# Convolution and attention on one core: bulk transfers on GpSimd's queue, 18 diagonal products in place of 36, norm sums a slot earlier

## The chip, the cores and the metric

The kernel runs on one core of a Trainium2 chip. The metric is the device time in microseconds (us); the time before is the median of three runs. A core has five engines with a queue of instructions each: PE (TensorE, matrix products), DVE (VectorE), ACT (ScalarE), POOL (GpSimd) and SP (SyncE, used here for transfers only). Transfers are issued from the queues of SP, ACT and POOL and are carried out by the core's 16 DMA engines.

## What is computed

The reference takes images x of 4 x 384 x 48 x 48 and does this (shortened):

```python
x_flat = x.reshape(B, C, N).transpose(0, 2, 1)
local = conv7x7_per_channel(x, conv_w) * inv + (bn_beta - bn_mean * inv)
x_norm = layernorm(x_flat)
q, k, v = heads(x_norm @ qkv_w.T + qkv_b)
q = q + heads(layernorm(local_flat))
attn = softmax(q @ k.T * 48 ** -0.5)
out = x_flat + (attn @ v) @ proj_w.T + proj_b
```

There are N = 2304 tokens of C = 384 channels in an image, and 8 heads of 48. So there are a depthwise convolution of 49 taps, two layer norms over channels, three projections, attention of every token with every token of its image, and an output projection with a residual.

## The kernel before

**Tiles.** An image is cut into six groups of 8 rows (384 tokens), so there are 24 tiles t = 6b + g. Heads are taken in four pairs. Channels lie on the partitions in three chunks of 128 (heads 0 to 5 fill 48 of each 64 rows, heads 6 and 7 fill the other 16 in thirds).

**Slots.** The attention of a tile has 12 slots, three for each pair of heads. A slot (`score_batch`, `weigh_batch`, lines 925 to 938) scores six blocks of 128 keys (`score`, line 897: six products of 64 rows each for a block, L902, then an exponential on ACT, L910) and weighs the values with the result (`weigh`, L917). After the last slot, `sums_out` copies the sums to SBUF on ACT (L802, L812) and `sums_add` adds the thirds on DVE (L821).

**Between images** comes a key stage: for each of six groups, `from_x` (line 588) projects values, keys and queries of the next image and the output of the image before (all L529). Keys are split in a high and a low part; `keys_out` (line 556) sends them in pieces, for pair 0 to the SBUF stack `ks` on SP's queue, for the others to `wide` in HBM on POOL's queue. `load_keys` (line 582, L586) brings a pair's keys back in thirds on POOL's queue; there are two `ks` buffers, and a load of the next pair waits until PE has read the last key of the pair before the present one.

**Convolution.** DVE does the taps (`conv_ops`, line 263; L289, the first one L285), one instruction for a tap and chunk. They run one tile ahead of attention. `plan` (line 377) spreads them over the points between other work: each point has an estimate of DVE's room there (`spare`, `spare_at_keys`) and each tile a due point (`due`). For the first two tiles some taps of chunk 0 are done on PE, as products with diagonals (`products`, L304): 10 taps for tile 0, `MORE_TAPS` for tile 1, whose diagonals `make_more` (line 312) writes into buffers that are not yet in use. Products stand ahead of an ACT copy into the accumulator (L1047), and after that come the first tile's `query_end`, `high_queries` and `low_queries`.

**Norms.** Class `Norm` sums over channels. In the first image's tiles the mean comes from PE (`mean_kept`). Elsewhere `sum` adds the chunks on DVE (L422, L423) and `out` (line 473) transposes, reduces, and sends the sums in two hops over HBM on SP's queue (`parts` L482, `four` L483), since the four partial sums lie on different partitions. `few_centre` and `few_variance` take them up on DVE (L492, L500, L506); then come the squares on ACT (L417, run in `weigh_batch` ahead of the weighing) and the same again for the variance. The norm of the local part of the next tile runs in slots `first - 1` to `second + 1` (5 and 8), that of the coming image's x around `X_SLOTS`.

**Queries.** `high_queries` rounds a pair's queries on ACT (L774), `low_queries` takes the difference on DVE (L779) and sends six hops within SBUF on SP's queue (L784, L786), after which the scores of that pair can start. `gather_tails` (line 531, L535) collects the tails of the queries for pair 3 in eight hops.

**Queues.** The order on PE, DVE and ACT is the order of the source. On SP and POOL the scheduler of the framework sets the order of transfers at build time, so it has to be read from the built kernel. On SP's queue there lie, beside the hops, the slabs of the convolution (`load_slab`), the tiles of x (`load_x`), the residuals (`load_residual`), and the outputs held in HBM until the key stage (`hold`, `fetch`). A finished tile is divided by its sums (`divide`, slot 2) and multiplied and held at `OUT_SLOT`.

Of the kernel before, what the change touches and what calls it, by code (L numbers as in the profile page):

```python
# [25 lines left out]
NSLOT = 12  # L26
X_SLOTS = 4, 7
X_LATER = 3
OUT_SLOT = 4
WARM = 14  # L30
PE_TAPS = 10
MORE_TAPS = 36

# [11 lines left out]
def unshifted_pass(  # L47
# [16 lines left out]
    nc = tc.nc  # L64
    B, C, N = x.shape
    W = 48
# [26 lines left out]
    def load_packed(dst, src, queue=nc.sync):  # L93
        for p0, piece in segments(src):
            queue.dma_start(out=dst[p0 : p0 + piece.shape[0]], in_=piece)
# [4 lines left out]
    def place_x(b, g):  # L100
        xn[b, g] = big.tile([P, CC, G], F32, tag=f"xn{g}", name=f"xn{b}_{g}")
        return xn[b, g]

    def load_x(b, g):
        load_packed(place_x(b, g), x[b, :, g * G : (g + 1) * G])

    slabs = {}

    def load_slab(b, g, parts=1):
        first, end = max(0, g * RG - PAD), min(H, (g + 1) * RG + PAD)  # L110
        t = work.tile([P, CC, (RG + 2 * PAD) * W], F32, tag="slab", name=f"slab{b}_{g}")

        edges = (first, (g + 1) * RG, end) if parts == 2 else (first, end)
        for a, e in zip(edges, edges[1:]):
            load_packed(t[:, :, (a - first) * W : (e - first) * W], x[b, :, a * W : e * W])
        slabs[b, g] = (t, first, end)


# [57 lines left out]
                    )  # L176

    load_by_pair(of_ln, ln_pair, (nc.scalar, nc.gpsimd))
    load_slab(0, 0, parts=2)
    place_x(0, 0)  # L180
    nc.gpsimd.tensor_scalar_add(inv, norms[:, 3], BN_EPS)
    nc.gpsimd.tensor_tensor(inv, inv, neg_half, ALU.pow)
# [50 lines left out]
    load_packed(staged[1], qkv_wT[:, C : 2 * C])  # L233
    load_packed(staged[0], qkv_wT[:, 0:C])
    for g in range(1, NG):
        load_x(0, g)
    load_by_pair(qk_vec, qk_b, (nc.gpsimd, nc.gpsimd))
    with nc.allow_non_contiguous_dma(reason="a few vectors, once"):
        load_packed(vbp, v_b.rearrange("o c -> c o"), nc.gpsimd)
# [70 lines left out]
        return more[i // 9][:, i % 9 * P : i % 9 * P + P]  # L310

    def make_more():
        for tag, bufs in (("qs", 5), ("qs", 5), ("ao", 2), ("rb", 1)):
            d = work.tile([P, CC, G], F32, tag=tag, name="more", bufs=bufs)
            more.append(d.rearrange("p c g -> p (c g)"))
            for i in range(9 * len(more) - 9, 9 * len(more)):
                nc.scalar.mul(more_diagonal(i), ident, cw[:, 0, taps[i] : taps[i] + 1])
            yield
# [5 lines left out]
    def norm_slots(t):  # L324
        return (8 - (t > 0), None) if t + 1 < NG else (5, 8)

    def spare(t, s, half):
        b, g = divmod(t, NG)
        first, second = norm_slots(t)
        time = 3.6 - (0.0 if half else 0.6) - (0.6 if half and s % 3 == 1 else 0.0)  # L330
        if b + 1 < B and g >= later(b + 1):
            time -= {(3, 1): 2.3, (4, 1): 2.2, (5, 1): 2.3, (7, 0): 0.4, (8, 0): 2.6}.get(
                (s, half), 0.0
            )
        if g:
            time -= {(2, 0): 0.7, (4, 1): 1.4}.get((s, half), 0.0)
        if t + 1 < NG:
            time -= {(first + 1, 0): 1.4, (first + 2, 0): 4.3, (first + 3, 0): 0.6}.get(
                (s, half), 0.0
            )  # L340
        elif g < NG - 1:
            time -= {(4, 1): 2.3, (5, 1): 2.2, (6, 1): 2.3, (8, 0): 0.4, (9, 0): 4.5}.get(
                (s, half), 0.0
            )
        return max(0.3, time)
# [23 lines left out]
    each = CC * KS * KS  # L369
    due = []  # L370
    for t in range(1, NT):
        last = ("slot", t - 1, norm_slots(t - 1)[0], t < NG) if t % NG else ("kv", t, 4, 0)
        due.append((points.index(last), t * each - MORE_TAPS))
    share = {}

# [279 lines left out]
    def both(making):  # L655
        next(making)
        next(making)

    def lows_out(n):
        for _ in range(n):  # L660
            lows.popleft()()
# [92 lines left out]
    def query_end(t):  # L754

        acc = accs.pop(t)
        q = xn[divmod(t, NG)]
        q3 = work.tile([P, G], F32, tag="qt", name=f"qt{t}", bufs=1)
        queries[t] = q, q3
        for c in range(CC):  # L760
            nc.vector.scalar_tensor_tensor(
                q[:, c, :], acc[:, c, :], gain[:, c : c + 1], q[:, c, :], ALU.mult, ALU.add
            )
# [7 lines left out]
    def high_queries(t, p):  # L771
        qs = work.tile([P, 3, G], HALF, tag="qs", name=f"qs{t}_{p}", bufs=5)
        stacked[t, p] = qs
        nc.scalar.copy(qs[:, 0, :], query_of(t, p))  # L774

    def low_queries(t, p):

        qs = stacked[t, p]
        nc.vector.tensor_sub(qs[:, 1, :], query_of(t, p), qs[:, 0, :])  # L779
        qs = qs.bitcast(F32)  # L780
        for j in range(2):
            r = 64 * j
            if p < CC:
                nc.sync.dma_start(out=qs[r + HD : r + 64, 0:2], in_=qs[r : r + 16, 0:2])  # L784
            for i in range(2):
                nc.sync.dma_start(  # L786
                    out=qs[r + 32 * i : r + 32 * i + 32, 2], in_=qs[r + 16 : r + HD, i]
                )
# [69 lines left out]
    def load_residual(t, tag="qs", bufs=5):  # L858
        b, g = divmod(t, NG)
        xr = work.tile([P, CC, G], F32, tag=tag, name=f"xr{t}", bufs=bufs)  # L860
        nc.sync.dma_start(
            out=xr, in_=x[b, :, g * G : (g + 1) * G].rearrange("(c p) n -> p c n", p=P)
        )
        residuals[t] = xr
# [2 lines left out]

    def hold(t):
        held[t] = dram.tile([P, CC, G], F32, tag=f"held{t % NG}", name=f"held{t}", bufs=1)
        nc.sync.dma_start(out=held[t], in_=outputs[t][0])  # L870

    def fetch(t):
        if t < NT - NG:
            ao = work.tile([P, CC, G], F32, tag="qs", name=f"af{t}", bufs=5)
        else:
            ao = big.tile([P, CC, G], F32, tag=f"xn{t % NG}", name=f"af{t}")
        nc.sync.dma_start(out=ao, in_=held[t])
        return ao

    def finish(t, co, m, queue=nc.sync):  # L880
# [44 lines left out]
    def score_batch(t, s):  # L925
        p, k0 = s // (KB // BATCH), s % (KB // BATCH) * BATCH
        for kb in range(k0, k0 + BATCH):
            score(t, p, kb)
# [17 lines left out]
    def convolve_first(n):  # L946
        nonlocal n_first
        n_first += n
        for _ in range(n):
            next(stream)  # L950
# [62 lines left out]
    for g in range(1, NG):  # L1013

        last = g == NG - 1
        next(making_more, None)
        making = from_x(0, g)
        both(making)
        assert not last or n_first >= each - PE_TAPS
        norm = Norm(accs[0] if last else xn[0, g + 1])  # L1020
        norm.mean_by_chunk(norm.src)
        if last:
            added = output_bias()
        convolve_first(4)
        norm.centre()
        norm.squares()
        both(making)
        if not last:
            convolve_first(4)
            both(making)  # L1030
        norm.mean_by_chunk(norm.buf)
        norm.root()
        lows_out(1)
        if last:
            both(making)
        both(making)
        convolve_first(6 if last else 10)
        if not last:
            lows_out(2)
        if last:  # L1040
            local_end(0, norm.newton())
        else:
            norm.scale(norm.newton())
        both(making)
        if not last:
            convolve_first(7)
    nc.scalar.activation(  # L1047
        accs[1][:, 0, :], products(1, MORE_TAPS, more_diagonal), AF.Identity, bias=shift[:, 0:1]
    )
    query_end(0)  # L1050
    high_queries(0, 0)
    low_queries(0, 0)
    lows_out(2)
    gather_tails(*reversed(queries[0]))
    nc.vector.tensor_add(pb, pb, added)
    plan(n_first - (each - PE_TAPS))

    for t in range(NT):
        b, g = divmod(t, NG)
        if g == 0 and b:  # L1060
# [4 lines left out]
            for gk in range(NG):  # L1065
# [40 lines left out]
                    norm.squares()  # L1106
                if gk == 5:
                    low_queries(t, 0)
                    gather_tails(*reversed(queries[t]))
                both(making)  # L1110
                convolve("kv", t, gk, 3)
                lows_out(2)
# [18 lines left out]
        for s in range(NSLOT):  # L1131
# [3 lines left out]
            if early and s == first + 3:  # L1135
                high_queries(t + 1, 0)
            score_batch(t, s)
            if pair < NP - 1 or g < NG - 1:
                load_keys(b, (pair + 1) % NP, third)
            if s == 1 and g == 0:  # L1140
# [29 lines left out]
                norm.few_variance()  # L1170
            if early and s == first + 3:
                low_queries(t + 1, 0)
                gather_tails(*reversed(queries[t + 1]))
            convolve("slot", t, s, 0)
            sums_add()
            if early and s == first + 1:
# [18 lines left out]
            convolve("slot", t, s, 1)  # L1195
            if following and s == second + 1:
                low_queries(t + 1, 0)
                gather_tails(*reversed(queries[t + 1]))
            if coming and s == X_SLOTS[0]:
                norm_x.few_centre()  # L1200
            if following and s == first:
# [1 line left out]
            if s == OUT_SLOT and g:  # L1203
                ao = outputs[t - 1][0]
                nc.vector.tensor_mul(ao, ao, rb)
                hold(t - 1)
            if coming and s == X_SLOTS[0] - 1:
                norm_x = Norm(xn[b + 1, g - later(b + 1)])
                norm_x.sum()
                norm_x.out()  # L1210
            if coming and s == X_SLOTS[0] + 1:
                norm_x.sum_squares()
                norm_x.out()
            if following and s == first - 1:
                norm = Norm(accs[t + 1])
                norm.sum()
                norm.out()
# [562 lines left out]
```

## Time and profile before

| what | us |
|---|---|
| median of three runs | 2858.78 |
| lowest and highest | 2855.7 and 2859.26 |
| the profiled execution: own time | 2871.85 |
| the profiled execution: span of its instructions | 2870.1 |
| PE busy in the span | 2802.3 |
| DVE busy | 2419.7 |
| ACT busy | 1653.8 |
| POOL busy | 592.4 |

The profile is of one execution, whose own time lies 13.1 us above the median. "PE" is the time in which products run, "PEld" the loading of weights beside it. A row of waits reads: engine, what it was to do and the line, what it waited for, total us, number of times, longest. A row of the timeline reads: start and length in us, engine, line, operation, output and inputs, number of records, and in brackets the idle time ahead of it with what ended it. SPq is the transfer queue of SP. A product of 32-bit floats shows as two records. The three key stages lie near 750, 1464 and 2150 us, the tiles' slots between them.

### The profile page before, as it was taken

What the parts mean: (1) busy time and instruction counts of PE and PEld (TensorE: products, weight loads), DVE (VectorE), ACT (ScalarE), POOL (GpSimd) and SP (SyncE); (2) the same over time, 40 slices, a digit from 0 to 9 for tenths busy, and PEclk for the clock granted to TensorE, in tenths of its full rate; (3) what the DMA queues carried; (4) which work ended last, traced back from release to release, by engine and by line L of the source; (5) the groups of instructions that cost most, each with busy time, mean ns of one, the idle gap of its engine ahead of it and who ended that gap; (6) DMA issues with size and microseconds to landing.
All of it is one profiled execution on the core that took longest, in us unless ns stands there. A gap on an engine that the chain in (4) does not pass through costs nothing.

```text
span 2870.1 us, 53777 instructions
## 1 busy us (share of the span) xinstructions
PE 2802.3 (98%) x19366; PEld 1757.3 (61%) x19366; DVE 2419.7 (84%) x4783; ACT 1653.8 (58%) x2677; POOL 592.4 (21%) x1125
## 2 busy tenths in 40 slices
PE   9999999999999998999999999999999999999999
PEld 6655666666655655655665566666565566666665
DVE  7759899989899887988989999989888999988502
ACT  5436666666424665666642476666662266666662
POOL 5720000000274100000036400001006610110000
PEclk9999999999999999999999999999999999999999
DMA  6434544554455444445545554454455545535541
GB/s 141 108 111 137 146 136 138 152 154 152 112 154 163 144 132 146 138 132 154 153 117 155 168 165 144 144 149 145 135 151 151 136 161 158 147 136 169 165 160 62
DMA packets 195348, 410.33 MB, mean 143 GB/s; under 512 B 67776, under 2 KB 138368, under 8 KB 194560
## 3 DMA queue, kind: packets, MB, share of 16 engines
q0 software_dynamic: 65440, 254.88, 26.4%
q1 hardware_dynamic: 126640, 148.30, 21.5%
q8 instruction: 155, 2.54, 0.4%
q10 hardware_dynamic: 2992, 3.62, 0.4%
q14 instruction: 121, 0.99, 0.1%
HBM read 298.25 MB, written 64.73 MB: 126 GB/s over the span
## 4 chain that ended last, share of the span: by engine, by line
PE 72%; DVE 15%; DMA 8%; ACT 1%; issue 1%; POOL 1%; SPq 1%; ACTq 0%; DVEq 0%
PE o L917 30%; PE r L902 25%; PE r L529 16%; DVE acc L289 9%; DMA four<-parts 2%; DMA qs<-qs 1%; DMA parts<-part 1%; PE r L304 1%; DVE sq L478 1%; DMA wide<-k 0%; DVE sq L423 0%; ACT pt L910 0%; DVE part L479 0%; DVE sq L422 0%; DMA slab<-in_x_dram 0%
## 5 line engine op out<-in xcount | busy, mean ns | idle before, releaser
L289 DVE SCALAR_TENSOR_TENSOR acc<-slab,vec,acc 128x368 f32<-128x368 f32 (+4 forms) x3412 | 1751.6, 585 | 1.6
L910 ACT ACTIVATE pt<-r 128x768 f32<-128x768 f32 x1728 | 1248.8, 829 | 115.8 <-PE r L902 92.0
L917 PE MATMUL o<-pt,v 128*64 128x384 f32 x6912 | 1181.9, 491 | 1.9 <-ACT pt L910 1.8
L902 PE MATMUL r<-qs,ks 64*128 64x384 f32 x10368 | 1010.6, 343 | 56.1 <-ACT ao L812 26.0
L902 PEld LDWEIGHTS r<-qs,ks 64*128 64x128 f32 x10368 | 900.7, 187 | 244.8 <-issue 178.6
L917 PEld LDWEIGHTS o<-pt,v 128*64 128x64 f32 x6912 | 471.5, 137 | 592.7 <-issue 515.2
L586 POOL DMA_DIRECT2D ks<-wide x276 | 199.3, 724 | 1811.6 <-PE r L902 1781.6
L802 ACT COPY o<-o 113x384 f32<-113x384 f32 x192 | 92.0, 479 | 388.5 <-PE o L917 388.5
L529 PE MATMUL r<-xn,w_qk 128*128 128x384 f32 x864 | 283.7, 486 | 0.0
L529 PEld LDWEIGHTS r<-xn,w_qk 128*128 128x128 f32 x864 | 164.2, 190 | 114.5
L529 PE MATMUL r<-w_v,xn 128*128 128x384 f32 x432 | 145.1, 488 | 0.5 <-ACT w_v L715 0.5
L606 ACT COPY v<-r 128x384 f32<-128x384 f32 x72 | 32.1, 480 | 186.2 <-PE r L529 186.2
L821 DVE TENSOR_TENSOR ao<-ao,o 113x384 f32<-113x384 f32 x144 | 79.7, 554 | 50.8 <-ACT o L802 50.5
L529 PE MATMUL r<-af,w_o 128*128 128x384 f32 x360 | 119.1, 487 | 0.0
L529 PEld LDWEIGHTS r<-w_v,xn 128*128 128x128 f32 x432 | 81.5, 190 | 59.1 <-issue 2.4
L492 DVE TENSOR_REDUCE few<-four 128x12 f32<-128x48 f32 x72 | 16.7, 232 | 117.1 <-DMA four<-parts 117.1
L812 ACT COPY ao<-o 113x384 f32<-113x384 f32 x72 | 34.4, 478 | 131.9 <-PE o L917 131.9
L529 PEld LDWEIGHTS r<-af,w_o 128*128 128x128 f32 x360 | 68.2, 190 | 47.8 <-issue 0.6
L554 POOL DMA_DIRECT2D wide<-k x192 | 96.5, 507 | 2.9 <-issue 2.6
L576 POOL DMA_DIRECT2D wide<-k x192 | 92.8, 489 | 11.4 <-DMA wide<-k 9.6
L570 POOL DMA_DIRECT2D wide<-k x144 | 70.8, 495 | 101.9 <-ACT k L614 70.1
L779 DVE TENSOR_TENSOR qs<-xn,qs 128x384 fp32r<-128x384 f32 x72 | 39.9, 554 | 55.9 <-ACT qs L774 55.8
(131 smaller groups left out, 1224.9 us busy)
## 6 DMA issues: line engine op xcount, KB each, us to landing
ks<-wide POOLq DMA_DIRECT2D x276, 768.0 KB, 6.8
qs<-qs SPq DMA_DIRECT2D x528, 48.0 KB
xr<-in_x_dram SPq DMA_DIRECT2D x24, 576.0 KB
slab<-in_x_dram SPq DMA_DIRECT2D x32, 378.0 KB
wide<-k POOLq DMA_DIRECT2D x480, 24.0 KB, 2.0
held<-ao SPq DMA_DIRECT2D x20, 576.0 KB
af<-held SPq DMA_DIRECT2D x20, 576.0 KB
rb<-rden SPq DMA_DIRECT2D x48, 216.0 KB
```

What stands on the lines that cost most here:

```text
L289: nc.vector.scalar_tensor_tensor(dst, src, weight, dst, ALU.mult, ALU.add)
L529: nc.tensor.matmul(dst, lhsT=weights(c), rhs=src(c), start=c == 0, stop=c == CC - 1)
L554: queue.dma_start(out=dst[r + 32 * i : r + 32 * i + 32, 1], in_=k[r + 16 : r + HD, 1])
L570: nc.gpsimd.dma_start(out=last[16 * u : 16 * u + 16, 0], in_=k[r : r + 16, 0])
L576: nc.gpsimd.dma_start(out=last[to : to + 16, 1], in_=k[r : r + 16, 1])
L586: nc.gpsimd.dma_start(out=stacks[b, p].bitcast(F32)[:, :, at], in_=wide[b, p][:, :, at])
L779: nc.vector.tensor_sub(qs[:, 1, :], query_of(t, p), qs[:, 0, :])
L802: nc.scalar.copy(part[0 : 64 + HA], sums[0 : 64 + HA, 0, :G])
L821: nc.vector.tensor_add(dst, dst, part[0 : 64 + HA])
L902: nc.tensor.matmul(r[:, j, :G], lhsT=ks[rows, w, kb * P : (kb + 1) * P], rhs=qs[rows, m, :], start=i == 0, stop=i == 2,)
L910: nc.scalar.activation(pt, r[:, :, :G], AF.Exp, scale=SCALE)
L917: nc.tensor.matmul(sums[halves[j], 0, :G], lhsT=values[t // NG, kb // NB][:, first : first + 64], rhs=pt[:, j, :], start=i == 0, stop=i == ...
```

## The change

Bulk transfers (slabs, x, residuals, held outputs) go from SP's queue to POOL's, except those of the start; the small hops, the denominators' broadcast (`rb`) and the output of finished tiles stay on SP. Tile 1 has 18 taps done as products in place of 36, and the first tile's query work stands ahead of these products. Both norms' first sums are formed one slot earlier, and the room estimates and due points follow. The tails are gathered in slot 0, after its scores, in place of directly after the first query hops. The finished tile is multiplied and held in slot 7 in place of 4. Below, the line with `dma_start` stands for the three of `load_residual`, `hold` and `fetch`; the block with `both(making)` is the end of the start-up; `gather_tails` is no longer called elsewhere.

```diff
-OUT_SLOT = 4
+OUT_SLOT = 7
-MORE_TAPS = 36
+MORE_TAPS = 18
...
-    def load_x(b, g):
-        load_packed(place_x(b, g), x[b, :, g * G : (g + 1) * G])
+    def load_x(b, g, queue=nc.gpsimd):
+        load_packed(place_x(b, g), x[b, :, g * G : (g + 1) * G], queue)
...
-    def load_slab(b, g, parts=1):
+    def load_slab(b, g, parts=1, queue=nc.gpsimd):
...
-    load_slab(0, 0, parts=2)
+    load_slab(0, 0, 2, nc.sync)
...
-        load_x(0, g)
+        load_x(0, g, nc.sync)
...
-        for tag, bufs in (("qs", 5), ("qs", 5), ("ao", 2), ("rb", 1)):
+        for tag, bufs in (("qs", 5), ("qs", 5)):
...
-            time -= {(3, 1): 2.3, (4, 1): 2.2, (5, 1): 2.3, (7, 0): 0.4, (8, 0): 2.6}.get(
+            time -= {(2, 1): 2.3, (4, 1): 2.2, (5, 1): 2.3, (7, 0): 0.4, (8, 0): 2.6}.get(
...
-            time -= {(2, 0): 0.7, (4, 1): 1.4}.get((s, half), 0.0)
+            time -= {(2, 0): 0.7, (7, 1): 1.4}.get((s, half), 0.0)
...
-            time -= {(4, 1): 2.3, (5, 1): 2.2, (6, 1): 2.3, (8, 0): 0.4, (9, 0): 4.5}.get(
+            time -= {(3, 1): 2.3, (5, 1): 2.2, (6, 1): 2.3, (8, 0): 0.4, (9, 0): 4.5}.get(
...
-        last = ("slot", t - 1, norm_slots(t - 1)[0], t < NG) if t % NG else ("kv", t, 4, 0)
+        last = ("slot", t - 1, norm_slots(t - 1)[0] - (t >= NG), t < NG) if t % NG else ("kv", t, 4, 0)
...
-        nc.sync.dma_start(
+        nc.gpsimd.dma_start(
...
-        both(making)
+        next(making)
+        if last:
+            query_end(0)
+            high_queries(0, 0)
+            low_queries(0, 0)
+        next(making)
         if not last:
             convolve_first(7)
+    lows_out(2)
     nc.scalar.activation(
         accs[1][:, 0, :], products(1, MORE_TAPS, more_diagonal), AF.Identity, bias=shift[:, 0:1]
     )
-    query_end(0)
-    high_queries(0, 0)
-    low_queries(0, 0)
-    lows_out(2)
-    gather_tails(*reversed(queries[0]))
...
             score_batch(t, s)
+            if s == 0:
+                gather_tails(*reversed(queries[t]))
...
-            if coming and s == X_SLOTS[0] - 1:
+            if coming and s == X_SLOTS[0] - 2:
                 norm_x = Norm(xn[b + 1, g - later(b + 1)])
...
-            if following and s == first - 1:
+            if following and s == first - 2:
                 norm = Norm(accs[t + 1])
```

More of the change, by code (lines that the diff above doesn't have):

```diff
@@ L114, in load_slab @@
         for a, e in zip(edges, edges[1:]):
-            load_packed(t[:, :, (a - first) * W : (e - first) * W], x[b, :, a * W : e * W])
+            load_packed(t[:, :, (a - first) * W : (e - first) * W], x[b, :, a * W : e * W], queue)
         slabs[b, g] = (t, first, end)
@@ L869, in hold @@
         held[t] = dram.tile([P, CC, G], F32, tag=f"held{t % NG}", name=f"held{t}", bufs=1)
-        nc.sync.dma_start(out=held[t], in_=outputs[t][0])
+        nc.gpsimd.dma_start(out=held[t], in_=outputs[t][0])
     def fetch(t):
@@ L876, in fetch @@
             ao = big.tile([P, CC, G], F32, tag=f"xn{t % NG}", name=f"af{t}")
-        nc.sync.dma_start(out=ao, in_=held[t])
+        nc.gpsimd.dma_start(out=ao, in_=held[t])
         return ao
@@ L1108, in unshifted_pass @@
                     low_queries(t, 0)
-                    gather_tails(*reversed(queries[t]))
                 both(making)
@@ L1172, in unshifted_pass @@
                 low_queries(t + 1, 0)
-                gather_tails(*reversed(queries[t + 1]))
             convolve("slot", t, s, 0)
@@ L1197, in unshifted_pass @@
                 low_queries(t + 1, 0)
-                gather_tails(*reversed(queries[t + 1]))
             if coming and s == X_SLOTS[0]:
```

## The prediction

> **What bounds the kernel now.** I began with the busy times and the waits of PE, because an engine that is busy for 98% of the span can only be sped up by less work or fewer pauses.
>
> ```profile
> PE 2802.3 (98%) x19366; PEld 1757.3 (61%) x19366; DVE 2419.7 (84%) x4783; ACT 1653.8 (58%) x2677; POOL 592.4 (21%) x1125
> ...
> PE r L902 <- ACT ao L812: 26.0, 7, 6.3
> PE r L902 <- DMA qs<-qs: 17.1, 11, 3.5
> PE r L902 <- issue: 4.9, 2, 4.1
> ...
> DVE few L492 <- DMA four<-parts: 117.1, 40, 11.9
> ACT sq L417 <- DVE acc L500: 41.3, 7, 8.5
> ```
>
> PE is the bound, with about 60 us of visible waits. The seven waits on L812 match the seven waits of ACT's squares (L417) on the centring L500, which matches DVE's waits for the hop `four`. The timeline of PE gives the undisturbed rhythm (a slot is 36 score records, then 24 weighing records, 7.36 us from one o group to the next), and what a pause costs beside its length:
>
> ```profile
> 193.19 3.41 PE L902 MATMUL r<-qs,ks 64*128 64x384 f32 x36
> ...
> 1041.03 3.41 PE L902 MATMUL r<-qs,ks 64*128 64x384 f32 x18 [5.15 <-ACT ao L812]
> ...
> 1104.91 5.30 PE L902 MATMUL r<-qs,ks 64*128 64x384 f32 x31 [3.55 <-DMA qs<-qs]
> ...
> 155.61 22.61 PE L304 MATMUL r<-slab,more 128*128 128x384 f32 x72
> 179.27 0.56 DVE L779 TENSOR_TENSOR qs<-xn,qs 128x384 fp32r<-128x384 f32 x1 [26.14 <-ACT qs L774]
> 183.68 5.56 PE L902 MATMUL r<-qs,ks 64*128 64x384 f32 x35 [0.69 <-DMA qs<-qs]
> ```
>
> After a long pause 18 score records take the 3.41 us that 36 need otherwise. And at 155 the 36 products stand in front of everything: the query cast waits for them on ACT, so DVE idles 26 us and PE has a hole after them. The DMA queue of SP around one stall shows why the hops are late:
>
> ```profile
> 1023.97 0.59 SPq L482 DMA_DIRECT2D parts<-part  x1
> 1024.61 0.79 SPq L95 DMA_DIRECT2D xn<-in_x_dram  x1
> 1030.39 0.58 SPq L483 DMA_DIRECT2D four<-parts  x1
> ...
> 1046.78 0.55 SPq L482 DMA_DIRECT2D parts<-part  x1
> 1047.43 1.55 SPq L786 DMA_DIRECT2D qs<-qs  x2
> 1049.08 0.58 SPq L483 DMA_DIRECT2D four<-parts  x1
> ```
>
> With bulk on the queue the first hop takes 6.4 us, without it 2.3.
>
> **What the Trainium skill says.** "TensorE: Matmul & The Clock Gate", What's actually happening: after an idle window of about 3.4 us the array runs at half clock until it has been busy about as long. The trace agrees: score records have a median of 332 ns and a maximum of 686, and the window 1070 to 1160, with three stalls, has a granted clock of 0.92. "DMA: Bandwidth & Descriptors", Queues, rings and completion order: each DMA engine takes turns between the queues it has work for, packet by packet. So a hop alone on its queue need not stand behind bulk on another. Same page, Issuing engines are not separate DMA queues: all queues share 16 engines, so moving bulk adds no bandwidth. The trace bears this in part: the hop `parts` issued on SP at 2106.65, 4.8 us after three key loads on POOL, takes 4.1 us, against 2.3 above. Same page, Specifications: the first byte takes about 1 us from GpSimd, 0.6 from SyncE; here POOL's small `wide<-k` lands in 2.0, so nothing is charged.
>
> **The change part by part.** All against the profiled span of 2870.1 us (own time 2871.85).
>
> *18 products in place of 36.* 72 records take 22.6 us, so 36 records less is 11.3 us on PE, on the path. The query cast, its difference and its hops now come before the products, so the hole after them closes: products ended at 178.2, the first o group began at 189.2, 11.0 later, and an undisturbed score batch takes 3.4: 7.6 us. Sum -18.9. The 18 taps go to DVE: the records follow each other every 0.51 us (14 in 7.22), 9.2 us. I cost them at nothing: DVE loses the 26.1 us wait and can start while PE does the 11 us of products. Worked through the plan's formulas, tile 0 gets 161 taps in place of 154, tile 1 154 for 150, tiles 2 and 3 three and two more. If that cover is gone, 9.2 us.
>
> *First slab on POOL's queue.* The built order puts the first piece of slab 1 (378 KB) ahead of the inverse deviation on POOL, before the weights; in the trace it left SP only at 32.7. From 9 to 36 us the DMA share is 1.0 or more at about 190 GB/s, and PE waits there for weights (1.1 us at 19.8). 378 KB at that rate is 2.0 us, all 1008 KB 5.3. I take +2.5, range 0 to +5.3.
>
> *Bulk off SP: the query hops.* Stalls put down to qs<-qs inside slots: the o groups at 290.3, 1110.1 and 1140.6 are late by 7.6, 6.5 and 8.3, 22.4 us with the slow clock. At 1091.7 four slab transfers stand ahead of six query hops that end 1104.8, 6.0 us after the last was issued; alone a hop takes 2.0 to 2.3, so it would land near 1101, when PE asks for it. I take the full -22.4; at least half if shared engines keep them at 4. The tail gather (eight hops, about 5 us of SP) moves behind the scores in the source, but the built order still hoists most of it, so nothing is booked.
>
> *Norm sums a slot sooner, with the same cure.* The seven stalls on L812 with their aftermath (o groups at 1044.4, 1244.4, 1340.3, 1928.9, 2026.3, 2526.6, 2618.3): 7.5, 9.9, 8.0, 5.6, 8.0, 3.4, 3.4, sum 45.7. `four` is awaited at most 11.9 us; it gets 7.36 more and two hops lose up to 4 each. -45.7. What is late next is DVE itself: near 1690 to 1870, undisturbed, it is busy 171 of 180 us, and the plan gives tile 6 five taps more (2.6 us). I charge +10 (three stalls of the small kind, 3.4), bounds 0 and +34 (half of both stall sums).
>
> *Bulk on POOL.* 20 + 20 + 24 held, fetched and residual tiles, 92 slab and 72 x pieces at 0.5 to 0.7 us are some 130 us of POOL, mostly in the 20 us per pair for which it waits for PE anyway (1781.6 in all). The built order sets slab and held transfers between the last third of one key load and the first of the next, or within a load that has three slots; a wait for DVE there costs nothing. In the key stages it has company: each transfer waits for the landing of the one eight places ahead, and 576 KB tiles now stand among key pieces. Key buffers are freed later; the first scores after 890 already pause 1.8 us for that. +3, +0.5, +0.5, so +4; bounds 0 and +24 (8 per stage).
>
> *Output at slot 7, later held copy:* nothing; the next buffer is asked for a tile later.
>
> Sum: -18.9 + 2.5 - 22.4 - 45.7 + 10 + 4 = -70.5, own time 2801.4. The profiled execution is 13.1 above the median of 2858.78; taken off, 2788. The floor, with all charges at nothing, is 2772.
>
> **Rivals.** *DVE takes over* (half of both stall sums returns as waits for late centrings): for it the 84% and the full window 360 to 449 (88.8 of 89 us), against it that PE did not pause in that window. 2788 - 10 + 34 = 2812. *Hops stay slow*, since the engines are shared: for it the 4.1 us at 2106.65. A third of the query stalls and a quarter of the others stay, 19 us instead of the 10: 2797. *The queue change does nothing*, only start-up gains: 2788 - 10 + 68 = 2846; against it the 2.3 us at 1046.8. *Slower: POOL paces the key stages.* A group lasts 140/6 = 23.3 us, POOL is busy 87.7/6 = 14.6, added issues 1.5, and 1.8 big tiles hold it w each. It is the bound from w = 4.0; the 18 groups eat the whole gain from w = 6.3. A key load lands in 6.8 and eight issues cover 4, so w is about 2.8; at 7 the groups last 28.7: 18 x 5.4 = 97, 2881.
>
> **How the numbers follow.** Forecast 0.50, DVE 0.18, slow hops 0.18, start-up only 0.07, POOL 0.05, unnamed 0.02 around no change. The measurement can tell about 0.2%, 6 us. Faster 0.93, within 0.02, slower 0.05. The range 2768 to 2818 holds the first three: floor less 4, to the DVE case and 6 more.
>
> **What would show it.** L304 at 36 records and no 26 us wait on L779; the first o group near 171 to 175; no PE wait on L812 above 2 us; DVE's wait for `four` below 40; granted clock 1.0 from the first slots on. Wrong if PE waits at key stages for `wide<-k`, if L779 or L500 stay late with the hops landed (DVE), or if weights at 20 us are late by over 5.

## The result and the profile after

The changed kernel takes 2808.32 us (median of 4 runs, 2800.62 to 2811.07) against 2857.34 for the kernel before on the same chip: a ratio of 0.9824 with a 95% interval of [0.9803, 0.9845]. Timed again later, the ratio was 0.9811 [0.9791, 0.9831]. So the change makes the kernel 1.8% faster. The forecast was 2788; the time lies inside the range of 2768 to 2818, 20 us above the forecast. The profiled execution of the changed kernel has an own time of 2808.18 and a span of 2806.1: here the profiled execution lies on the median.

The rows of the page and of the waits that answer to those of before:

```profile
PE 2773.0 (99%) x19330; PEld 1747.7 (62%) x19330; DVE 2430.9 (87%) x4801; ACT 1648.4 (59%) x2659; POOL 729.7 (26%) x1353
```

```profile
DVE few L492 <- DMA four<-parts: 33.5, 14, 5.1
...
PE r L902 <- DMA qs<-qs: 9.1, 7, 2.4
PE r L902 <- issue: 7.4, 2, 4.9
```

PE's waits for the squares (L812, 26.0 us before) are gone from the list, and DVE waits for `four` 33.5 us in place of 117.1. The waits for query hops have halved. PE is busy 29 us less: 11 us are the products left out, and 15 us the same 10368 score records (1010.6 us before, 995.4 now), of which fewer run at the slow clock after a pause (mean granted clock 0.990 before, 0.995 now). The timeline of PE at the end of the start-up:

```profile
158.43 11.42 PE L304 MATMUL r<-slab,more 128*128 128x384 f32 x36
169.78 3.39 PE L902 MATMUL r<-qs,ks 64*128 64x384 f32 x36
173.10 4.09 PE L917 MATMUL o<-pt,v 128*64 128x384 f32 x24
```

The products are 36 records, the scores follow them without a hole and at full speed (36 in 3.39 us), and the first o group starts at 173.1 in place of 189.2. The hop that answers to the one at 1023.97 before, and what POOL's queue sends next:

```profile
1002.06 0.60 SPq L482 DMA_DIRECT2D parts<-part  x1
1004.10 0.58 SPq L483 DMA_DIRECT2D four<-parts  x1
...
1006.34 2.19 POOL L95 DMA_DIRECT2D xn<-in_x_dram  x4 [16.75 <-DVE qs L779]
1009.49 2.19 POOL L586 DMA_DIRECT2D ks<-wide  x3 [0.95 <-PE r L902]
```

The second hop goes out 2.0 us after the first, in place of 6.4. No bulk is on SP's queue, and, sent a slot sooner, the hop is also through before the next key loads leave. So this place does not tell the queue from the slot; the experiments do.

What became of each pause is read from the starts of the o groups (an o group is the 24 weighing records of a slot). An undisturbed group starts 7.36 us after the one before it; "other stops" below sums what is above that, without the key stages, without the stop between tiles 0 and 1, and without the 2.1 and 3.3 us that the mean products add in tiles 0 to 4. "Key stages" is the time from the last o group ahead of each to the first behind it, all three together; a pause one slot later counts as another stop.

| profiled execution | own time | first o group | tiles 0 to 1 | key stages | other stops |
|---|---|---|---|---|---|
| before | 2871.85 | 189.2 | 7.4 | 448.1 | 63.5 |
| changed | 2808.18 | 173.1 | 6.3 | 460.1 | 5.3 |

The differences, -16.1, -1.1, +12.0 and -58.2, add up to -63.4; the own times differ by 63.7. The medians differ by 49 only.

### The profile page after: what moved, and what is told of

Its sections match the earlier page's. It is cut to its first block, busy times and chain, and to the rows that moved or that the text cites. A ratio compares the mean times of both kernels' runs of the same rounds, so it can differ in the third digit from the quotient of the medians.

```text
span 2806.1 us, 53985 instructions
## 1 busy us (share of the span) xinstructions
PE 2773.0 (99%) x19330; PEld 1747.7 (62%) x19330; DVE 2430.9 (87%) x4801; ACT 1648.4 (59%) x2659; POOL 729.7 (26%) x1353
## 4 chain that ended last, share of the span: by engine, by line
PE 87%; DVE 6%; DMA 3%; POOL 1%; issue 1%; ACT 1%; SPq 0%; DVEq 0%; ACTq 0%; POOLq 0%
PE o L917 39%; PE r L902 33%; PE r L529 14%; DVE acc L289 3%; DMA qs<-qs 1%; PE r L304 1%; DMA parts<-part 1%; DMA wide<-k 1%; POOL wide L554 0%; DMA four<-parts 0%; DVE k L617 0%; DMA ks<-k 0%; DMA rd<-den 0%; DVE xn L761 0%; DVE xr L883 0%
## 5 line engine op out<-in xcount | busy, mean ns | idle before, releaser
L289 DVE SCALAR_TENSOR_TENSOR acc<-slab,vec,acc 128x368 f32<-128x368 f32 (+7 forms) x3430 | 1762.5, 586 | 2.2
L902 PE MATMUL r<-qs,ks 64*128 64x384 f32 x10368 | 995.4, 341 | 20.3 <-DMA qs<-qs 9.1
L812 ACT COPY ao<-o 113x384 f32<-113x384 f32 x72 | 34.6, 481 | 139.7 <-PE o L917 139.7
L95 POOL DMA_DIRECT2D slab<-in_x_dram x92 | 55.6, 613 | 222.6 <-DVE acc L289 216.7
L95 POOL DMA_DIRECT2D xn<-in_x_dram x72 | 39.5, 557 | 212.5 <-DVE qs L779 212.5
```

The source lines that it names most:

```text
L289: nc.vector.scalar_tensor_tensor(dst, src, weight, dst, ALU.mult, ALU.add)
L902: nc.tensor.matmul(r[:, j, :G], lhsT=ks[rows, w, kb * P : (kb + 1) * P], rhs=qs[rows, m, :], start=i == 0, stop=i == 2,)
```

## The experiments

**How the runs are compared.** Ratios are to the kernel before, run beside it on the same chip. The kernels are variants of the changed one, but for `e0_before`. The columns are those of the table above.

| run | ratio [95%] | median | first o group | tiles 0 to 1 | key stages | other stops |
|---|---|---|---|---|---|---|
| e0_before | - | 2860.41 (one run) | 190.2 | 8.4 | 450.1 | 48.0 |
| e1_bulk_on_sp | 0.9809 [0.979, 0.9827] | 2806.08 | 170.1 | 7.4 | 449.1 | 11.4 |
| e2_norm_later | 0.9964 [0.9953, 0.9976] | 2852.06 | 172.7 | 7.3 | 457.1 | 52.9 |
| e3_36_products | 0.9882 [0.9863, 0.9902] | 2827.81 | 192.6 | 8.2 | 457.2 | 8.3 |
| e4_outputs_on_sp | 0.9798 [0.9785, 0.9811] | 2798.0 | 172.1 | 6.2 | 453.6 | 1.3 |
| e5_slabs_on_sp | 0.9795 [0.9783, 0.9808] | 2798.96 | 170.7 | 6.9 | 450.2 | 5.4 |
| e6_products_only | 0.9934 [0.9919, 0.9948] | 2836.84 | 169.6 | 7.2 | 449.0 | 45.2 |
| e7_extra_bulk | 0.9913 [0.9898, 0.9928] | 2831.38 | 172.1 | 7.1 | 464.3 | 20.2 |
| e8_x_on_pool | 0.9809 [0.9791, 0.9826] | 2801.61 | 170.4 | 6.7 | 452.8 | 9.5 |
| e9_early_queries | 0.9787 [0.9767, 0.9807] | 2795.47 | 171.3 | 0 | 447.2 | 15.0 |
| e10_both | 0.9775 [0.9757, 0.9793] | 2792.93 | 171.1 | 0 | 452.4 | 6.9 |
| e11_after_again | 0.9811 [0.9791, 0.9831] | 2807.04 | 172.7 | 7.5 | 456.4 | 6.6 |

**The kernel before, once more (e0_before).** No edit.

> The kernel before, unchanged, profiled once more. The first profiled execution took 2871.85, 13 us more than the timed runs, and my forecast took these 13 us off again. Theory A: the number and size of PE's short stops differ from one execution to the next, so a second profiled execution can lie anywhere between 2855 and 2872, with correspondingly fewer late o groups. Theory B: the profiler slows this kernel down: again 2868 to 2874 with the same late o groups.

Its profiled execution took 2860.41, 11.4 us less than the first, with other stops of 48.0 in place of 63.5. In the list of waits of this run the row for the squares has four entries, not seven:

```profile
PE r L902 <- DMA qs<-qs: 18.8, 12, 3.3
PE r L902 <- ACT ao L812: 15.5, 4, 4.7
```

Theory A holds. The timed runs of the kernel before also spread from 2854.95 to 2869.3 in that series. The second profiled execution lies near the median, and the 11.4 us between the two are more stops of the very kind that the change removes.

**Bulk back on SyncE's queue (e1_bulk_on_sp).**

```diff
-    def load_x(b, g, queue=nc.gpsimd):
+    def load_x(b, g, queue=nc.sync):
-    def load_slab(b, g, parts=1, queue=nc.gpsimd):
+    def load_slab(b, g, parts=1, queue=nc.sync):
...
-        nc.gpsimd.dma_start(
+        nc.sync.dma_start(
             out=xr, in_=x[b, :, g * G : (g + 1) * G].rearrange("(c p) n -> p c n", p=P)
         )
...
-        nc.gpsimd.dma_start(out=held[t], in_=outputs[t][0])
+        nc.sync.dma_start(out=held[t], in_=outputs[t][0])
...
-        nc.gpsimd.dma_start(out=ao, in_=held[t])
+        nc.sync.dma_start(out=ao, in_=held[t])
```

> The changed kernel with all bulk transfers back on SyncE's queue; products and norm sums stay as changed. Theory A: the queue part is worth little on balance. The stops at query hops come back (+11), the first slab no longer delays the weights (-3), the key stages get back their 150 us (-12): 2801 to 2808. Theory B (the forecast): the queue part cures the hops and hardly costs anything in the key stages: the query stops return in full (22) and a part of the stops at the squares too, as both hops of a sum take 4 us more: 2825 to 2835.

0.9809 against 0.9811 and 0.9824 for the changed kernel: on balance the queue part is worth nothing that can be told from zero. Theory A holds for the time. The first o group is 3.0 us earlier, the key stages are back at 449 us, and other stops grow by some 6 us: one is 6.9 at a query hop, and one of 3.7 directly after the first key stage takes back a part of what that stage gained. The stops at the squares do not return.

**Norm sums in their old slots (e2_norm_later).**

```diff
-OUT_SLOT = 7
+OUT_SLOT = 4
...
-            time -= {(2, 1): 2.3, (4, 1): 2.2, (5, 1): 2.3, (7, 0): 0.4, (8, 0): 2.6}.get(
+            time -= {(3, 1): 2.3, (4, 1): 2.2, (5, 1): 2.3, (7, 0): 0.4, (8, 0): 2.6}.get(
...
-            time -= {(2, 0): 0.7, (7, 1): 1.4}.get((s, half), 0.0)
+            time -= {(2, 0): 0.7, (4, 1): 1.4}.get((s, half), 0.0)
...
-            time -= {(3, 1): 2.3, (5, 1): 2.2, (6, 1): 2.3, (8, 0): 0.4, (9, 0): 4.5}.get(
+            time -= {(4, 1): 2.3, (5, 1): 2.2, (6, 1): 2.3, (8, 0): 0.4, (9, 0): 4.5}.get(
...
-        last = ("slot", t - 1, norm_slots(t - 1)[0] - (t >= NG), t < NG) if t % NG else ("kv", t, 4, 0)
+        last = ("slot", t - 1, norm_slots(t - 1)[0], t < NG) if t % NG else ("kv", t, 4, 0)
...
-            if coming and s == X_SLOTS[0] - 2:
+            if coming and s == X_SLOTS[0] - 1:
...
-            if following and s == first - 2:
+            if following and s == first - 1:
```

> The changed kernel with the norm sums in their old slots (room, due points and output slot too); bulk stays on GpSimd's queue. Theory A: either cure alone is enough for the stops at the squares: two hops of a sum save 4 us each, more than the 3 to 6 us for which PE waited, so 2805 to 2811, with no wait of PE on L812 over 2 us. Theory B: the slot is what cures them, as hops stay at 4 us beside bulk on the shared engines: half of the 45.7 us returns, 2825 to 2835.

My theory A fell, and B's direction was too small: nearly the whole gain at the squares went, 0.0146 of the ratio (from the mean of the two for the changed kernel), which is 42 us. The run puts room estimates, due points and the output slot back together with the sums, so the 42 us are those of the whole set. PE waits on L812 seven times again, 23.7 us in all. The timeline around the longest shows why a queue of its own does not save the hop:

```profile
1206.44 0.58 POOL L870 DMA_DIRECT2D held<-ao  x1 [6.72 <-DVE ao L1205]
...
1207.57 2.19 POOL L586 DMA_DIRECT2D ks<-wide  x3
1208.44 0.59 SPq L482 DMA_DIRECT2D parts<-part  x1
1216.85 0.58 SPq L483 DMA_DIRECT2D four<-parts  x1
1219.01 0.23 DVE L492 TENSOR_REDUCE few<-four 128x12 f32<-128x48 f32 x1 [7.04 <-DMA four<-parts]
...
1223.04 3.41 PE L902 MATMUL r<-qs,ks 64*128 64x384 f32 x18 [8.36 <-ACT ao L812]
```

SP's queue has nothing ahead of `parts`, yet `four`, which waits for it, goes out 8.4 us later. In these 8.4 us the three key loads (2.3 MB) issued on GpSimd's queue are in flight; the last of them was issued at 1209.04 and lands 7.8 us later, as `four` goes out.

**36 products and the old order of the start (e3_36_products).**

```diff
-MORE_TAPS = 18
+MORE_TAPS = 36
...
-        for tag, bufs in (("qs", 5), ("qs", 5)):
+        for tag, bufs in (("qs", 5), ("qs", 5), ("ao", 2), ("rb", 1)):
...
-        next(making)
-        if last:
-            query_end(0)
-            high_queries(0, 0)
-            low_queries(0, 0)
-        next(making)
+        both(making)
...
+    query_end(0)
+    high_queries(0, 0)
+    low_queries(0, 0)
     lows_out(2)
     nc.vector.tensor_add(pb, pb, added)
```

> The changed kernel with 36 products for tile 1 and the query work behind them, as before. Theory A: the start costs 18.9 us again and nothing is given back later, so 2824 to 2830. Theory B: the 18 taps less for VectorE in the first two tiles end the stop of 6.3 us between tiles 0 and 1, so 2816 to 2822.

Theory A holds: 0.9882 less 0.9818 is 0.0064, 18.4 us, and the stop between tiles 0 and 1 is still there (8.2 us). The 18 taps that VectorE took over cost nothing that shows.

**The outputs alone back on SyncE's queue (e4_outputs_on_sp).** The last three pairs of lines of the diff of e1.

> The changed kernel with only the residuals and the held and fetched outputs back on SyncE's queue; slabs and x stay on GpSimd's. Theory A: the key stages are longer because slab pieces on a queue of their own go out ahead of the last query hops and fill the shared DMA engines, so nothing returns: key stages stay at 155, 155 and 151, time 2805 to 2811. Theory B (as the forecast had it): the 576 KB residuals and outputs hold up the key pieces on GpSimd's queue; key stages fall to 150, time 2796 to 2800.

**The slabs alone (e5_slabs_on_sp).** The second pair of lines of that diff.

> The changed kernel with only the slabs back on SyncE's queue, the first one of tile 1 too; x, residuals and outputs stay on GpSimd's. Theory A: slab pieces queue behind the query hops again, so key stages fall to about 150 each (-11), and the start gains 3; some query stops return (+4): 2796 to 2803. Theory B: it is residuals and outputs that lengthen the key stages: only the start gains, 2803 to 2807.

Both come out near 0.980, some 6 us below the changed kernel, but their intervals overlap both of its intervals, so a gain is not shown. In e4 the time is B's and the first key stage A's, so neither theory holds alone; in e5 the time is A's. With the outputs on SP the first key stage stays long (154.8 us) and the second and third fall to 149.7 and 149.1; with the slabs on SP the first falls too, to 151.2. For that first one the traces suggest a cause. The changed kernel at the end of the first key stage:

```profile
868.25 1.63 POOL L95 DMA_DIRECT2D slab<-in_x_dram  x3
...
870.85 0.54 SPq L784 DMA_DIRECT2D qs<-qs  x1
...
873.33 0.55 SPq L786 DMA_DIRECT2D qs<-qs  x1
...
877.67 0.66 PE L902 MATMUL r<-qs,ks 64*128 64x384 f32 x1 [4.92 <-issue]
```

and e5_slabs_on_sp at the same place:

```profile
871.46 0.59 SPq L786 DMA_DIRECT2D qs<-qs  x1
872.10 1.53 SPq L95 DMA_DIRECT2D slab<-in_x_dram  x3
...
872.32 0.41 PE L902 MATMUL r<-qs,ks 64*128 64x384 f32 x1 [1.40 <-issue]
```

On one queue the slab pieces stand behind the query hops; on a queue of their own they go out ahead of them, and PE waits 4.92 us in place of 1.40. The link is read from the order, as "issue" names no releaser; but all six profiles with slabs on GpSimd's queue (the changed kernel twice, e2, e3, e4, e7) have a first stage of 154.8 us or more, and all six with slabs on SyncE's 152.5 or less. Most of this is only moved: behind the shorter stage PE pauses one slot later, 1.8 us in e5 and 2.0 to 5.3 in e1, e6, e8, e9 and e10, where the changed kernel has none. With that pause counted, the first stage takes 153.0 to 155.4 us with slabs on SyncE's queue and 154.8 to 156.4 on GpSimd's (159.6 in e7, which adds bulk). The chain of work that ends last shows both cases: in e5 and e1 it runs through the key pieces `wide<-k` on GpSimd's queue, which take 5.2 and 5.9 us to land and whose buffers the exponentials of that slot need; in the changed kernel it runs through a query hop that takes 5.9. The second stage needed no cure: its 154.7 in the changed kernel was that execution's, as the same kernel has 150.1 in e11.

**The products alone (e6_products_only).** The diffs of e1 and e2 together.

> The kernel before with the 18 products and the early query work alone; bulk on SyncE's queue and norm sums in their old slots. Theory A: this part is worth its 19 us in any company, and with sums in their old slots the queue change costs about 10: 2838 to 2843, below the 2852 of the kernel that has the queue change too. Theory B: the queue change does cure part of the stops where sums are late: then this kernel lies above 2852, at 2855 to 2860.

The median of 2836.84 lies a little under A's range, but below e2 as A had it, and the intervals do not touch. This run completes a square, from which each part's worth follows (the difference of the ratios by the median of 2858.78 us):

| | bulk on SyncE's queue | bulk on GpSimd's queue | queue part |
|---|---|---|---|
| sums in their old slots | 0.9934 (e6) | 0.9964 (e2) | +8.6 us (± 5) |
| sums a slot sooner | 0.9809 (e1) | 0.9818 (changed, mean of two) | +2.6 us (not told from 0) |
| worth of the sooner sums | -35.7 us (± 7) | -41.7 us | |

The products, with the early query work, are worth 1 - 0.9934, 18.9 us. The tails gathered in slot 0 are in this run and in every other variant, so their part is not separated. Why the queue costs 8.6 us where the sums are late was not isolated. One candidate is the order on GpSimd's queue: in the lines of e2 above, the key loads stand behind a held output that waited 6.72 us for VectorE, and then meet the hop.

**One more bulk copy at each sum (e7_extra_bulk).**

```diff
+            extra = dram.tile([P, CC, G], F32, tag="extra", name="extra")
+            nc.scalar.dma_start(
+                out=extra, in_=x[0, :, 0:G].rearrange("(c p) n -> p c n", p=P)
+            )
             nc.sync.dma_start(out=parts.rearrange("i q k -> q i k"), in_=part)
```

> The changed kernel with added work: at each of the 72 norm sums ScalarE's queue sends one more copy of 576 KB from HBM to HBM, which nobody reads. Theory A: the DMA engines are shared, so the hop of the sums, alone on its queue, goes from its 2.2 us (median) to 4 or more; waits for the sums grow from 33 us to over 80 and some stops of PE return: 2815 to 2840. Theory B: a hop alone on its queue is served in turn with the bulk of other queues: its median stays below 2.7, and the time within 2806 to 2812.

The time is 2831.38, as A had it. The hop was sized too high. DVE's wait for it, at L496 in this variant, grew to 52.4 us, not over 80:

```profile
DVE few L496 <- DMA four<-parts: 52.4, 23, 6.6
```

From the issue of `parts` to that of `four` the median of the 72 goes from 2.2 to 3.3 us. Part of the loss is not the hop: many slots with an added issue on ACT are 0.2 to 0.3 us longer. So bulk on a third queue slows a hop that is alone on its own.

**All but the next image's x back on SyncE's queue (e8_x_on_pool).** The diff of e1 without its first pair.

> The changed kernel with slabs, residuals and outputs back on SyncE's queue, so that only the next image's x stays on GpSimd's. Theory A: each of these two took about 9 us off by itself because it ends the same loss in the second and third key stage; together they add only the 5 us of the first: 2793 to 2799. Theory B: they add up, 2808 - 10 - 9: 2786 to 2791. Theory C: a fuller SyncE queue makes query hops late as in the kernel with all bulk there: 2802 to 2808.

0.9809: the gains seen in e4 and e5 do not add up. The time lies between A and C, and the interval overlaps those of e4, e5 and the changed kernel, so nothing is told apart here.

**First queries sent earlier (e9_early_queries).** The slab line of e1, and:

```diff
             for r in (0, 64):
-                nc.sync.dma_start(
+                nc.gpsimd.dma_start(
                     out=dst[r + 16 * i : r + 16 * i + 16], in_=src[r + HD : r + 64, c, :]
                 )
...
-            if early and s == first + 3:
-                high_queries(t + 1, 0)
             score_batch(t, s)
...
-            if early and s == first + 3:
-                low_queries(t + 1, 0)
             convolve("slot", t, s, 0)
...
+            if early and s == first + 2:
+                high_queries(t + 1, 0)
             weigh_batch(t, s)
+            if early and s == first + 2:
+                low_queries(t + 1, 0)
```

> The changed kernel with slabs on SyncE's queue, the gather of tails on GpSimd's, and the first queries of the next tile rounded and sent half a slot earlier in tiles 0 to 4 of the first image. Theory A: the last stop common to all kernels, some 7 us between tiles 0 and 1, is a hop that starts 3 us too late and meets key loads; sent earlier it goes: 2789 to 2795. Theory B: the hops meet other transfers or VectorE waits for the rounding, so the stop moves only: 2797 to 2803.

**The same with the outputs on SyncE's queue (e10_both).** The diffs of e4 and e9 together.

> The same as the kernel with early queries, and residuals and outputs on SyncE's queue too. Theory A: 2786 to 2793, at best the sum of both. Theory B: no better than either, 2795 to 2800.

In both the stop between tiles 0 and 1 is gone. The changed kernel there:

```profile
253.24 4.94 SPq L535 DMA_DIRECT2D qt<-xn  x8
258.29 0.52 SPq L786 DMA_DIRECT2D qs<-qs  x1
...
259.83 2.16 POOL L586 DMA_DIRECT2D ks<-wide  x3 [19.77 <-PE r L902]
...
265.76 0.62 PE L902 MATMUL r<-qs,ks 64*128 64x384 f32 x4 [1.85 <-DMA qs<-qs]
```

and e10_both:

```profile
252.57 0.51 SPq L786 DMA_DIRECT2D qs<-qs  x1
...
257.84 2.22 POOL L586 DMA_DIRECT2D ks<-wide  x3 [1.87 <-PE r L902]
...
261.48 3.41 PE L902 MATMUL r<-qs,ks 64*128 64x384 f32 x36
```

The six query hops are out before the key loads begin, and PE scores without a pause. Two edits act together here: the earlier rounding, and the tail gather, which no longer takes 4.94 us of SP's queue ahead of the hops; they were not separated. e9 comes out just above A's range (2795.47; a stop of 4.9 us appears at another hop, near 991, and one of 5.3 after the first key stage); e10 reaches A's upper end at 2792.93. Its interval does not touch the first one of the changed kernel, 0.9803 to 0.9845, and overlaps that of the repeat by 0.0002: by the ratios it is about 12 us faster than the changed kernel, and has the lowest ratio of all.

**The changed kernel once more (e11_after_again).** No edit.

> The changed kernel, unchanged, timed and profiled once more. Theory A: what its first profile showed is the rule and not one execution's luck: key stages together 455 to 461 us against 448 to 452 with bulk on SyncE's queue, a stop near 7 us between tiles 0 and 1, other stops under 15 us in sum, time 2803 to 2811. Theory B: the long key stages and the stop near 1109 are accidents of one execution: key stages at 450, time 2796 to 2802, no slower than the kernels that have part of the bulk on SyncE's queue.

Theory A holds for the time, 2807.04, and for the sum of the key stages (456.4). But only the first stage is long in both executions (154.8 and 155.8); the second went from 154.7 to 150.1. The stop near 1109 is smaller here, 1.5 us in place of 4.7: such stops wander from one execution to the next.

## Why the prediction was right in direction and 20 us too low

*18 products: right.* Forecast -18.9, measured -18.9 (e6, with the tails moved too) and -18.4 (e3). The hole after the products closed, as the three lines from 158.43 on show. The cover that I named for the 18 taps held.

*First slab on POOL's queue: right.* Forecast +2.5. In the profiles the first o group starts at 169.6 to 171.3 in the six kernels with this load on SP (e1, e5, e6, e8, e9, e10), at 172.1 to 173.1 in the five with it on POOL and 18 products: the means differ by 2.0 us. The trace has 201 GB/s in the window of 9 to 36 us, not the 190 of the forecast; that changes its 2.0 us by 0.1.

*Norm sums a slot sooner: right, and it is the slot, not the queue.* In the profile all seven stops went, -45.7 as forecast. I had named the queue as a second cure; e2 shows that it is none. In timed runs the slot is worth 36 to 42 us, for the reason under the last point.

*Bulk off SP, query hops, -22.4 in full: this step failed.* The three stops went from 7.4 (7.6 in the forecast), 6.5 and 8.3 to 6.3, nothing and 4.7, half of the sum; e11 has 7.5 in the first place. Even this half is not shown to be the queue's: with bulk back on SP (e1) the last two places have no stop either, but another query hop has one of 6.9. The rival with slow hops had the mechanism. The one in which the queue change does nothing was right about the queue, but it had tied the slot's worth to it, and the slot holds alone. My reason was what the Trainium skill says in "DMA: Bandwidth & Descriptors", Queues, rings and completion order, on taking turns. The taking of turns may well happen, though no run here shows it, but it does not protect a hop. I had also misread the stall at 1023.97. Besides the bulk on SP's queue, key loads were going out there on POOL's queue, which they use in both kernels:

```profile
1023.03 0.72 POOL L586 DMA_DIRECT2D ks<-wide  x1 [19.91 <-PE r L902]
1026.39 1.44 POOL L586 DMA_DIRECT2D ks<-wide  x2 [2.64 <-issue]
```

At 1046.78, where the hop took 2.3 us, there are none. Three key loads also left at 275.91, 1096.71 and 1125.32, amid the query hops of the three stops. So the 6.4 us against 2.3 were not the worth of an empty queue, and moving the other bulk could not take the key loads away.

Over the 72 sum hops of the changed kernel, from `parts` to `four` (pieces of up to 72 KB left out): 36 with under 300 KB issued on POOL since 9 us before have a median of 2.04 us, 33 with 1 MB or more have 4.58 and up to 8.94. For 18 of these 33 SP's queue had nothing over 72 KB either: 3.72, and up to 8.93. In the kernel before, 22 with bulk on SP and little on POOL had 4.04 (23 in e0: 3.3). So the bulk in flight counts more than its queue. In the changed kernel 31 of the hops went out with bulk of POOL's queue still in flight ahead of them; they took 2.0 to 8.9 us, and every one of them ended between 1.3 us before and 2.1 us after the landing of the last such transfer. The other 41 took 2.0 to 2.8. So a hop ended about as if it stood behind the bulk on one common queue. Bulk issued behind a hop can delay it too: the longest, 10.93 us in e2, had three key loads issued 0.2 us after it and ended 5.8 us after the bulk ahead had landed. What the same page says under Issuing engines are not separate DMA queues is borne out by e7. I quoted this, and the 4.1 us at 2106.65, and still took the hop at 2.3.

*The charge of +10 for new lateness: not needed.* Other stops are 5.3 us in all, and 4.7 of these are a query hop that was counted above. VectorE took over nowhere: PE waits for it once, for 1.0 us. The charge and the failed step nearly cancel, by luck: -12.4 forecast, -11.2 measured.

*Bulk on POOL in the key stages, +4: about right in size, not in its reason.* With the pause of 2.1 after the first stage of before, the key stages went from 450.2 to 460.1, +9.9; the two repeats, e11 against e0 (452.2 with its pause), give +4.2. The four profiles with all this bulk on POOL (the changed kernel twice, e2, e3) have 456.4 to 460.1, and the two with 18 products and all of it on SP (e1, e6) 452.9 and 454.3 with the pause: again about +4. But it is not POOL's pace: within a stage of the changed kernel PE has no pause over 1 us, only at its end, where in the first stage the query hops land behind slab pieces.

*The 13.1 us taken off at the end: this step failed, and is the largest part of the miss.* Against its own execution the sum was nearly right: 2801.4 forecast, 2808.2 measured. Then I took off that the profiled execution was above the median, as if that were the same overhead in both kernels. It was made of stops, 63.5 us of others in that execution against 48.0 in e0's, and I had already taken all of these away. They were counted twice. The changed kernel has few such stops left, so its profiled execution lies on its median. The Trainium skill notes, in "TensorE: Matmul & The Clock Gate", What's actually happening, that the cost of warming up differs from run to run as its window runs freely; in this case the number of stops differs too, seven and four at the squares.

Of the signs that the prediction named, these came true: 36 records at L304, no 26 us wait on L779 (the longest is 9.8), the first o group at 171 to 175, no wait on L812, and `four` below 40 us. The granted clock came near 1.0 but not fully: it is 0.97 from 240 to 300 us, at the stop between tiles 0 and 1, and 0.995 in all.

## What to carry to other kernels

A small transfer can be late through bulk in flight on any queue; give it time ahead (a slot sooner), or send it before the bulk, rather than a queue of its own. Moving bulk to a second queue also gives up an order: what stood behind the hops now goes out ahead of them, though here that moved a pause more than it made one. Before a slow transfer is laid to its own queue, look at what all the other queues have in flight. When a profiled execution lies above the median, ask what its surplus is made of before taking it off: if it is the stops that the change removes, it goes only once.

## What was not expected of the hardware

A hop of 6 KB with no bulk on its own queue took up to 8.93 us (10.93 in e2) with key loads of 768 KB and other bulk in flight on another queue, against 2.04 without; it ended about when the bulk issued ahead of it had landed, though that was on another queue. And executions of the same kernel differed by 14 us (2854.95 to 2869.3); in the two that were profiled the difference lies in the number and size of pauses.
